# A four-layer graph kernel on one core: the last rows leave in four transfers, attention's bias sum may run on either of two engines, and the planner's search gets other settings

## The chip, the cores and the metric

The kernel runs on one core of a Trainium2 chip. The core has five engines with a queue of instructions each: TensorE (PE; its weight loads are shown as PEld), VectorE (DVE), ScalarE (ACT), GpSimd (POOL) and SyncE (SP), which here only issues DMA transfers. Each engine runs its queue in order and waits on semaphores for what other engines make. SBUF is the on-chip memory of 128 partitions, PSUM holds matmul results in eight banks. The metric is the device time of one execution in microseconds (us), the median over several runs.

## The reference

The input x holds 128 graphs of 64 nodes with 256 features in float32, adj an adjacency matrix per graph. Four layers follow one another; each adds its result to its input and normalises the rows.

```python
# layer 0, gated recurrent steps, l = 0..4; A = (adj != 0)
m = h @ weight[l];  agg = A^T @ m;  h = gru_cell(agg, h)
x = layernorm(x + h * mask)
# layer 1, two-layer perceptron with RMS norm
agg = epsilon * x + adj @ x
x = layernorm(x + silu(rmsnorm(agg @ W1 + b1) * w) @ W2 + b2)
# layer 2, hyperbolic: log map, sum over neighbours, exp map, projection
x = layernorm(x + project(expmap0(adj @ logmap0(x))))
# layer 3, attention over neighbours
h = x @ W_w^T + W_b
u = adj * exp(e_i + f_j + a_b);  a = u / sum(u)
x = layernorm(x + a @ h)
```

## The kernel before, in words

Two graphs share the 128 partitions as a block, four blocks make a group, and 16 groups make the input. A group's rows are a tile of 128 x 4 x 256. Three sets of buffers let groups overlap. The program of a group is written by `group(g)` (from L612) as a stream of operations, each with the engine, an estimated duration and the buffers that it reads and writes; a buffer may be split into parts such as the four blocks. Nothing is emitted there. A planner, `Flow`, orders the streams of all groups and then emits every instruction; it ties each to the one before it on its engine, so that the order of every queue is the plan's.

The planner keeps several plans at once. `advance` (L79) extends one plan until its TensorE clock passes a limit: at each step it looks at the first operations of up to four consecutive streams (`WINDOW`), works out when each could start, and takes the earliest. An operation with two ways (`either`, L180) stands in both engines' queues, and its key is its start plus what that way costs more than the cheapest:

```python
key = (t + o.ways[e][0] - min(w[0] for w in o.ways.values()) if len(o.ways) > 1 else t, *rank(s, o))
```

Equal starts are settled by a rank. There are three: the earlier stream first; the later stream first (loads aside); and a rank that weighs a stream's number by `LAG` against the operation's longest remaining path in its own stream (`way`). `issue` (L231) extends every kept plan by a stretch of `STRETCH` us with every rank, sorts the results by `bound()` (L133, an estimate of the time at which such a plan can end: TensorE's lost time plus all of its work, or the longest remaining path), and keeps the best `WIDTH` of them. When less than `ENDGAME` us of TensorE's work are left, stretches are half as long and three times as many plans are kept. The planner knows hops between engines, the eight banks and the DMA's rate. It has no term for one engine holding up another's access to memory, or for TensorE's clock.

The steps that the change and the prediction name are these. `layer_norm` (L668) takes row statistics per block (`st` L673, `mv` L674), adds epsilon (`ve` L676), raises to the power -1/2 on GpSimd (`rstd` L678), makes an offset (`off` L684) and writes the four blocks of the result with `scaled` (L352), each block on ScalarE (L354) or VectorE (L355). In layer 1, GpSimd adds the second bias to the rows (`xb`, L853, 128 x 1024 elements), the projection `ps_o` is the last large matmul work of a group, and `xb` L959 adds it to the rows. Layer 2 makes the logarithm's factor on VectorE with a series (L983), sums over neighbours (`ps_sup`), and adds the result (`y`, L1028). Layer 3 transposes the rows (`ps_T`), multiplies by the attention weights (`ps_a`), scales by the exponentials (`hw`, L1045 to L1050), adds the bias to the rows on VectorE (L1052, 128 x 1024 elements), multiplies with the adjacency (`ps_att`), and for each block divides by the sum (`rd`, L1058 to L1060) and adds to the rows (`y`, L1061). The last norm's four blocks leave in one transfer, issued by SP (L1065):

```python
dve(1030, lambda: nc.vector.tensor_add(x3.tile(), x3.tile(), over(wb_r.tile(), NB)), [x3], [x3, wb_r])
flow.op("SP", 0.1, lambda: nc.sync.dma_start(out_rows[g], o.tile()), (), [o])
```

Of the kernel before, what the change touches and what calls it, by code (L numbers as in the profile page):

```python
# [14 lines left out]
OP = mybir.AluOpType  # L15
# [128 lines left out]
class Flow:  # L144
# [15 lines left out]

    DMA = (2.0, 330.0, 1.0)
    TRANSFERS = 8
    WINDOW, STRETCH, WIDTH, LAG = 4, 25.0, 8, 40.0


    ENDGAME = 350.0

    BEHIND = mybir.DependencyInfo(mybir.DependencyClass.NoSync, mybir.DependencyReason.DATA)

# [60 lines left out]

    def issue(self):  # L231
        self.ways()
        ranks = (lambda s, o: (s, o.n), lambda s, o: (s if o.kb else -s, o.n), lambda s, o: (self.LAG * s - o.way, s, o.n))
        plans, until = [Plan(self)], 0.0
        while any(p.left for p in plans):
            late = until > self.work - self.ENDGAME
            until += self.STRETCH / 2 if late else self.STRETCH
            found = {}
            for p in plans:
                for rank in ranks:  # L240
                    c = p.copy()
                    if c.advance(until, rank):
                        found.setdefault((round(c.bound(), 3), c.left), c)
            plans = [found[k] for k in sorted(found)[:self.WIDTH * (3 if late else 1)]]
        p, parts = plans[0], []
        past = (p.past, p.order)
        while past is not None:
            parts.append(past[1])
            past = past[0]
        last = {}  # L250
        for part in reversed(parts):
            for eng, o in part:
                made = o.ways[eng][1]()
                for i in made if isinstance(made, list) else [made]:
                    if eng in last:
                        self.tc.add_manual_dep(i.ins, last[eng].ins.name, self.BEHIND, reason="the plan's order")
                    last[eng] = i
# [3 lines left out]
def kernel(  # L261
# [31 lines left out]
    nc = tc.nc  # L293
# [4 lines left out]
    NB = 4  # L298
# [4 lines left out]
    NG = B // G  # L303
# [9 lines left out]
    flow = Flow(tc)  # L313
# [27 lines left out]
    def dve(n, run, w, r):  # L341
        flow.op("DVE", 0.16 + 0.00105 * n, run, w, r)
# [18 lines left out]
    out_rows = out.rearrange("(g b t) n d -> g (t n) b d", b=NB, t=2)  # L361
# [11 lines left out]
    def over(t, n):  # L373
        return t.unsqueeze(1).to_broadcast([P, n, t.shape[-1]])
# [192 lines left out]
    def everywhere(v, n, name, t=None):  # L567
        t = t or fixed([P, n], name)
        flow.op("POOL", 0.55, lambda: nc.gpsimd.dma_start(
            t.tile(), bass.AP(tensor=v.tensor, offset=v.offset, ap=[[0, P], [1, n]])), [t], kb=n / 2)  # L570
        return t
# [3 lines left out]
    wb_r = everywhere(att_b, D, "wb_r")  # L575
# [36 lines left out]
    def group(g):  # L612
        s = g % NF

        def tiny(name, shape=(P, NB), dt=F32):
            t = f"{name}{s}"
            return Buf(lambda: small.tile(list(shape), dt, tag=t, name=f"{name}_{g}"), slot=(t, 2))
# [4 lines left out]
        def rows(tag, name):  # L622
            return u(tag, name, (P, NB, D))
# [44 lines left out]
        def layer_norm(y, tag, name, norm=None):  # L668

            st, mv = tiny("st", (P, NB, 6)), tiny("mv", (P, NB, 2))  # L670
            ve, rstd = tiny("ve", (P, 2, NB)), tiny("rstd", (P, 2, NB))
            for b in range(NB):
                dve(256, lambda b=b: nc.vector.bn_stats(st[:, b, :], y[:, b, :]), [(st, b)], [(y, b)])  # L673
                dve(4, lambda b=b: nc.vector.bn_aggr(mv[:, b, :], st[:, b, :]), [(mv, b)], [(st, b)])  # L674
            m = 2 if norm else 1
            dve(4, lambda: nc.vector.tensor_tensor(  # L676
                ve[:, :m, :], over(mv[:, :, 1], m), eps2[:, :m, :], OP.add), [ve], [mv])
            pool(1.1, lambda: nc.gpsimd.tensor_tensor(rstd[:, :m, :], ve[:, :m, :], pow2[:, :m, :], OP.pow), [rstd], [ve])  # L678
            if norm:
                dve(4, lambda: nc.vector.scalar_tensor_tensor(  # L680
                    norm.tile(), rstd[:, 1, :], float(np.sqrt(D)), rstd[:, 0, :], OP.mult, OP.mult), [norm], [rstd])
            o = rows(tag, f"x_{name}")
            off = tiny("off")
            dve(4, lambda: nc.vector.scalar_tensor_tensor(  # L684
                off.tile(), mv[:, :, 0], -1.0, rstd[:, 0, :], OP.mult, OP.mult), [off], [mv, rstd])
            for b in range(NB):
                scaled(256, lambda b=b: o[:, b, :], lambda b=b: y[:, b, :], lambda b=b: rstd[:, 0, b:b + 1],
                       lambda b=b: off[:, b:b + 1], [(o, b)], [(y, b), off, rstd])
            return o
# [18 lines left out]
        for t in range(2):  # L708
            q = quads[t]
# [122 lines left out]
        for n in range(2):  # L832
            ps = rows_of(hT, n)
            for j in range(2):
                b = 2 * n + j
# [5 lines left out]
        for t in range(2):  # L841
            q = quads[t]
# [17 lines left out]
        def chunk(c):  # L860
            return hid[c // 2][:, c % 2, :], [(hid[c // 2], (c % 2, n)) for n in range(2)]
# [76 lines left out]
        for c in range(KH):  # L938
            v, parts = chunk(c)
# [9 lines left out]
        for h in range(NB // 2):  # L949
            ps = bank("ps_o1")  # L950
            for j in range(2):
                b = 2 * h + j
# [4 lines left out]
            for j in range(2):  # L957
                b = 2 * h + j
# [38 lines left out]
        us = tiny("ss")  # L997
        sup = [bank("ps_sup") for _ in range(NB // 2)]
        for h in range(NB // 2):
            for j in range(2):  # L1000
                b = 2 * h + j
                pe(256, lambda b=b, j=j, ps=sup[h]: matmul(
                    ps[:, j * D:(j + 1) * D], adjT[:, b, :], tan[:, b, :], 0, 1), [sup[h]], [adjT, (tan, b)])
            for j in range(2):
                b = 2 * h + j
# [25 lines left out]
        x3 = layer_norm(y2, "B", "n2")  # L1031
# [8 lines left out]
        for b in range(NB):  # L1040
            ps = bank("ps_a")
            for k in range(KD):
# [6 lines left out]
                    hw[:, b, :D], ps[:, :D], AF.Identity, scale=hw[:, b, D:D + 1])),  # L1049
                ("DVE", 0.43, lambda ps=ps, b=b: nc.vector.tensor_scalar(  # L1050
                    hw[:, b, :D], ps[:, :D], hw[:, b, D:D + 1], None, OP.mult))], [(hw, b)], [ps, (hw, b)])
        dve(1030, lambda: nc.vector.tensor_add(x3.tile(), x3.tile(), over(wb_r.tile(), NB)), [x3], [x3, wb_r])  # L1052
        y3 = rows("y", "y3")
        rd = tiny("rd")
        for b in range(NB):
# [6 lines left out]
                y3[:, b, :], ps[:, :D], rd[:, b:b + 1], x3[:, b, :], OP.mult, OP.add),  # L1062
                [(y3, b)], [ps, (rd, b), (x3, b)])
        o = layer_norm(y3, "A", "n3")
        flow.op("SP", 0.1, lambda: nc.sync.dma_start(out_rows[g], o.tile()), (), [o])  # L1065

    for g in range(NG):
        flow.stream()
        group(g)
# [33 lines left out]
```

## Time and profile before

| | |
|---|---|
| median of 4 runs | 2431.53 us (2430.47 to 2432.34) |
| profiled execution, own time | 2432.88 us |
| its span, first to last instruction | 2431.1 us |
| TensorE busy | 2397.1 us (99%) |
| VectorE busy | 1892.3 us (78%) |
| ScalarE busy | 1148.0 us (47%) |
| GpSimd busy | 188.4 us (8%) |
| mean granted TensorE clock | 0.994 |
| transfers out | 16 of 512 KB, 2.9 us from issue to landing |

Times in the profile are counted from the start of the span. A line of the timeline gives start, duration, engine, line of the kernel, operation, output and inputs, shapes, and how many instructions were merged; in brackets stands how long the engine had been idle before it, and what ended that. An overlap of a few hundredths between neighbours on one engine is the pipelining of the records. The granted clock is the share of full speed that the throttle gave TensorE.

### The profile page before, as it was taken

The page shows a single profiled execution, that of the slowest core. Times are in us where ns is not written, and L with a number is a line of the kernel's source. Part 1 is how long each engine was busy: PE and PEld are TensorE (multiplying, and loading weights), DVE is VectorE, ACT ScalarE, POOL GpSimd, SP SyncE. Part 2 cuts the span into 40 slices and gives each one's busy share as a digit, 9 for nine tenths or more (in the row PEclk, how much of TensorE's full clock was granted, in tenths as well). Part 3 has the DMA queues.
Part 4 walks back from the last instruction along what each step waited for, and adds up shares of the span by engine and source line. Part 5 has one row for each costly group of instructions (what it writes and reads, how often), then busy time and mean ns, then how long its engine had stood idle before and what let it go on. Part 6 is the DMA issues. An engine that isn't in the chain of part 4 may idle for free.

```text
span 2431.1 us, 32703 instructions
## 1 busy us (share of the span) xinstructions
PE 2397.1 (99%) x12258; PEld 2104.9 (87%) x12258; DVE 1892.3 (78%) x4097; ACT 1148.0 (47%) x2408; POOL 188.4 (8%) x144
## 2 busy tenths in 40 slices
PE   9999999999999999999999999999999999999996
PEld 7888888888888888888888888888888888888864
DVE  3668787887888877778777887788787787878777
ACT  4434544444444444454444545455444544445453
POOL 4000000000100000000000100000000000000011
PEclk9999999999999999999999999999999999999997
DMA  4000000000000000000000000000000000000000
GB/s 127 3 1 12 1 29 1 18 12 1 29 1 27 3 18 11 1 27 3 17 13 1 29 1 27 3 20 10 1 29 1 18 12 1 27 9 18 9 9 18
DMA packets 39725, 36.21 MB, mean 15 GB/s; under 512 B 9956, under 2 KB 38656, under 8 KB 39568
## 3 DMA queue, kind: packets, MB, share of 16 engines
q1 hardware_dynamic: 37840, 32.25, 4.2%
q8 instruction: 97, 1.59, 0.3%
q10 hardware_dynamic: 1328, 1.31, 0.2%
q0 software_dynamic: 400, 0.57, 0.1%
q14 instruction: 60, 0.49, 0.1%
HBM read 25.74 MB, written 8.39 MB: 14 GB/s over the span
## 4 chain that ended last, share of the span: by engine, by line
PE 94%; DVE 4%; DMA 1%; ACT 1%; issue 0%; POOL 0%; ACTq 0%; POOLq 0%; SPq 0%; DVEq 0%
PE p_v L663 11%; PE p_w L663 11%; PE p_in L663 11%; PE p_r L663 11%; PE p_hn L663 11%; PE ps_o L333 9%; PE ps_agg L333 6%; PE p_u L663 6%; PE ps_hr L643 3%; PE ps_a L333 2%; PE p_wh L882 2%; PE p_vh L882 2%; PE p_1h L882 2%; PE ps_T L633 1%; PE ps_att L333 1%; PE p_uh L882 1%
## 5 line engine op out<-in xcount | busy, mean ns | idle before, releaser
L663 PE MATMUL p_hn<-hT,w_hn 128*128 128x256 f32 x1280 | 322.8, 380 | 0.0
L663 PE MATMUL p_in<-agg,w_in 128*128 128x256 f32 x1280 | 315.3, 379 | 0.0
L663 PEld LDWEIGHTS p_in<-agg,w_in 128*128 128x128 f32 x1280 | 240.2, 190 | 31.1
L663 PEld LDWEIGHTS p_hn<-hT,w_hn 128*128 128x128 f32 x1280 | 227.9, 191 | 22.7
L333 PE MATMUL ps_o<-w2s,hid 128*128 128x256 f32 x1024 | 231.2, 379 | 0.0
L333 PEld LDWEIGHTS ps_o<-w2s,hid 128*128 128x128 f32 x1024 | 193.9, 190 | 27.3 <-issue 1.2
L678 POOL TENSOR_TENSOR rstd<-ve,pow 128x4 f32<-128x4 f32 (+1 forms) x64 | 82.6, 1291 | 1492.1 <-DVE ve L676 1484.4
L767 ACT ACTIVATE V<-V,half_b 128x256 f32<-128x256 f32 x160 | 72.7, 499 | 199.1 <-DVE V L763 198.9
L663 PE MATMUL p_u<-tA,s 128*128 128x256 f32 x640 | 158.1, 381 | 1.4 <-DVE tA L746 0.6
L663 PE MATMUL p_w<-tA,s 128*128 128x256 f32 x640 | 158.1, 379 | 0.0
L663 PE MATMUL p_r<-hT,a 128*128 128x256 f32 x640 | 156.9, 379 | 0.0
L663 PE MATMUL p_r<-agg,a 128*128 128x256 f32 x640 | 156.7, 379 | 0.0
L663 PE MATMUL p_v<-tB,s 128*128 128x256 f32 x640 | 155.4, 379 | 0.0
L663 PE MATMUL p_v<-tB,na 128*128 128x256 f32 x640 | 154.5, 379 | 0.0
L663 PE MATMUL p_w<-hT,s 128*128 128x256 f32 x640 | 154.3, 379 | 0.0
L349 ACT COPY agg<-ps_agg 128x512 f32<-128x512 f32 x154 | 90.0, 585 | 114.1 <-PE ps_agg L333 98.8
L333 PEld LDWEIGHTS ps_agg<-edge,hr 128*128 128x128 f32 x1024 | 136.1, 191 | 6.6
L354 ACT ACTIVATE hnb<-p_hn,half_b 128x256 f32<-128x256 f32 x232 | 101.8, 473 | 81.4 <-PE p_hn L663 67.4
L333 PE MATMUL ps_agg<-edge,hr 128*128 128x128 f32 x1024 | 138.8, 275 | 0.0
L663 PEld LDWEIGHTS p_u<-tA,s 128*128 128x128 f32 x640 | 119.3, 190 | 21.0 <-DVE tA L746 2.3
L663 PEld LDWEIGHTS p_v<-tB,s 128*128 128x128 f32 x640 | 120.9, 190 | 16.3 <-PE ps_att L333 0.2
L663 PEld LDWEIGHTS p_w<-hT,s 128*128 128x128 f32 x640 | 120.7, 190 | 16.0
(233 smaller groups left out, 4688.0 us busy)
## 6 DMA issues: line engine op xcount, KB each, us to landing
x<-in_x_dram SPq DMA_DIRECT2D x16, 512.0 KB, 3.7
xr<-in_x_dram SPq DMA_DIRECT2D x16, 512.0 KB, 3.6
out_dram<-x_n SPq DMA_DIRECT2D x16, 512.0 KB, 2.9
edge<-in_adj_dram SPq DMA_DIRECT2D x32, 64.0 KB, 2.3
wm<-in_L_gnn_weight_dram SPq DMA_DIRECT2D x5, 256.0 KB, 5.2
w2s<-in_L_gnn_W_dram SPq DMA_DIRECT2D x1, 1024.0 KB, 10.0
w<-in_L_gnn_W_dram SPq DMA_DIRECT2D x2, 512.0 KB, 3.5
w_in_L_gnn_w_hh_dram<-in_L_gnn_w_hh_dram ACTq DMA_DIRECT2D x1, 512.0 KB, 5.5
```

The lines of the kernel that those rows point to most:

```text
L333: return nc.tensor.matmul(o, lhsT, rhs, start=(k == 0), stop=(k == nk - 1))
L349: flow.either([("ACT", 0.27 + 0.00077 * n, lambda: nc.scalar.copy(o(), i())), ("DVE", 0.16 + 0.00105 * n, lambda: nc.vector.tensor_copy(o( ...
L354: flow.either([("ACT", 0.27 + 0.00077 * n, lambda: nc.scalar.activation(o(), i(), AF.Identity, bias=bias(), scale=scale())), ("DVE", 0.16 ...
L633: turn(lambda j=j, c=c: nc.tensor.transpose(ps[:, c * HR + j * P:c * HR + (j + 1) * P], src[:, 2 * n + j, c * P:(c + 1) * P], ident.tile() ...
L643: turn(lambda j=j, c=c: nc.tensor.transpose(ps[:, j * D + c * P:j * D + (c + 1) * P], src[:, c, (2 * n + j) * P:(2 * n + j + 1) * P], iden ...
L663: pe(256, lambda c=c, k=k: nc.tensor.matmul(ps[:, c * HR:(c + 1) * HR], w[:, k, c * P:(c + 1) * P], v(k), start=first and c == k == 0, sto ...
L678: pool(1.1, lambda: nc.gpsimd.tensor_tensor(rstd[:, :m, :], ve[:, :m, :], pow2[:, :m, :], OP.pow), [rstd], [ve])
L767: act(256, lambda c=c: nc.scalar.activation(o[:, c, :], src(c), AF.Tanh, bias=half_b[:, i * KD + c:i * KD + c + 1], scale=0.5), [(o, c)], ...
L882: pe(256, lambda c=c: nc.tensor.matmul(ps[:, c * HR:(c + 1) * HR], w1f[:, w, (2 * q + c) * P:(2 * q + c + 1) * P], v[0](), start=first and ...
```

## The change

There are three parts. In the last group each of the four blocks leaves by a transfer of its own, which waits for that block only; the other groups' rows still leave in one. Attention's bias sum becomes an operation with two ways, VectorE (estimated at 1.24 us) or GpSimd (2.35 us), and the planner takes one of them for each group. In the search, the lag rank's weight becomes 60 (as a list with one entry), the number of plans 6, and the last part begins 200 us of TensorE work before the end, with stretches of 6 us and 32 plans.

```diff
-    WINDOW, STRETCH, WIDTH, LAG = 4, 25.0, 8, 40.0
-    ENDGAME = 350.0
+    WINDOW, STRETCH, WIDTH, LAGS = 4, 25.0, 6, (60.0,)
+    ENDGAME, LAST_STRETCH, LAST_WIDTH = 200.0, 6.0, 32
...
-        ranks = (lambda s, o: (s, o.n), lambda s, o: (s if o.kb else -s, o.n), lambda s, o: (self.LAG * s - o.way, s, o.n))
+        ranks = (lambda s, o: (s, o.n), lambda s, o: (s if o.kb else -s, o.n), *(lambda s, o, lag=lag: (lag * s - o.way, s, o.n) for lag in self.LAGS))
...
             late = until > self.work - self.ENDGAME
-            until += self.STRETCH / 2 if late else self.STRETCH
+            until += self.LAST_STRETCH if late else self.STRETCH
...
-            plans = [found[k] for k in sorted(found)[:self.WIDTH * (3 if late else 1)]]
+            plans = [found[k] for k in sorted(found)[:self.LAST_WIDTH if late else self.WIDTH]]
...
-        dve(1030, lambda: nc.vector.tensor_add(x3.tile(), x3.tile(), over(wb_r.tile(), NB)), [x3], [x3, wb_r])
+        flow.either([(e, us, lambda v=v: v.tensor_tensor(x3.tile(), x3.tile(), over(wb_r.tile(), NB), OP.add))
+                     for e, us, v in (("DVE", 1.24, nc.vector), ("POOL", 2.35, nc.gpsimd))], [x3], [x3, wb_r])
...
-        flow.op("SP", 0.1, lambda: nc.sync.dma_start(out_rows[g], o.tile()), (), [o])
+        for q in [slice(0, NB)] if g < NG - 1 else [slice(b, b + 1) for b in range(NB)]:
+            flow.op("SP", 0.1, lambda q=q: nc.sync.dma_start(out_rows[g, :, q, :], o[:, q, :]), (),
+                    [(o, b) for b in range(q.start, q.stop)])
```

## The prediction

> **What bounds the kernel now.** I read the page's first two parts, then busy time by stretches, then the waits of TensorE, then the last 130 us instruction by instruction.
>
> The page, busy time of each engine and the 40 slices of the span:
>
> ```profile
> PE 2397.1 (99%) x12258; PEld 2104.9 (87%) x12258; DVE 1892.3 (78%) x4097; ACT 1148.0 (47%) x2408; POOL 188.4 (8%) x144
> ...
> PE   9999999999999999999999999999999999999996
> ...
> PEclk9999999999999999999999999999999999999997
> ```
>
> TensorE works 2397.1 of 2431.1 us. All that an order of work can change is the other 34.0 us, and the matmuls that run at a lower clock. The view by stretches tells where those are (columns: stretch, its length, PE, PEld, DVE, ACT, POOL, granted clock, DMA):
>
> ```profile
> 1000.00:1400.00 400.00, 400.00 (x2080) 355.81 (x2079) 319.25 (x699) 195.07 (x413) 27.90 (x19) 1.00 0.04 14
> 1800.00:2200.00 400.00, 399.45 (x2071) 354.58 (x2070) 319.15 (x677) 191.28 (x397) 27.79 (x19) 1.00 0.04 12
> ...
> 2300.00:2350.00 50.00, 46.03 (x185) 30.35 (x184) 35.78 (x63) 26.64 (x49) 7.56 (x4) 0.97 0.04 11
> ```
>
> ```profile
> 2384.10:2402.10 18.00, 7.54 (x17) 5.05 (x16) 14.91 (x74) 8.44 (x27) 4.66 (x4) 0.67 0.00 1
> 2402.10:2417.80 15.70, 15.24 (x64) 12.59 (x64) 12.54 (x43) 9.26 (x23) 1.56 (x1) 0.83 0.00 1
> ```
>
> Between 200 and 2200 us TensorE idles 2.8 us in five stretches of 400; the first 50 us hold 3.0. From 2300 us on it idles 28: 4.0 up to 2350, 10.5 after its last projection (2384.1) up to 2402.1, 13.3 after its last matmul (2417.8). From 2384.1 on the last two groups run their hyperbolic step, attention and norms side by side, a chain of small VectorE steps: VectorE is busy 33.55 of the 40.4 us up to 2424.5, so 6.9 us of it are free. The clock drops to 0.67: the eight records of ps_sup take 3.75 us, where eight records of the same size take 1.73 us in mid-run.
>
> What made TensorE wait around 2305 and 2337, from the timeline:
>
> ```profile
> 2301.78 2.73 DVE L786 SCALAR_TENSOR_TENSOR hT<-V,hT 128x512 f32<-128x512 f32 x1
> ...
> 2333.73 3.44 DVE L870 TENSOR_TENSOR sqs<-sqs,sq 128x512 f32<-128x512 f32 x2
> ...
> 2305.38 0.63 PE L643 MATMUL ps_hr<-ident,hT 128*128 128x128 f32 x4 [1.44 <-DVE hT L788]
> ...
> 2337.92 4.33 PE L333 MATMUL ps_hid<-aggm,w 128*128 128x512 f32 x6 [2.53 <-DVE aggm L350]
> ```
>
> ```profile
> 2301.48 2.48 POOL L853 TENSOR_TENSOR xb<-x_n,b_r 128x1024 f32<-128x1024 f32 x1 [1.63 <-ACT x_n L354]
> ...
> 2333.95 2.67 POOL L853 TENSOR_TENSOR xb<-x_n,b_r 128x1024 f32<-128x1024 f32 x1 [1.75 <-DVE x_n L355]
> ```
>
> While GpSimd adds 128x1024 elements, a VectorE operation of 0.69 us takes 2.73, and a pair of 1.48 takes 3.44. All 4.0 us of TensorE's idling before 2350 follow from that. This bears on the change, which may put 16 more adds of that size on GpSimd. The two adds it is about, and the end:
>
> ```profile
> 2406.10 1.22 DVE L1052 TENSOR_TENSOR x_n<-x_n,wb_r 128x1024 f32<-128x1024 f32 x1
> 2406.63 1.56 POOL L678 TENSOR_TENSOR rstd<-ve,pow 128x4 f32<-128x4 f32 x1 [5.51 <-DVE ve L676]
> ...
> 2412.13 1.23 DVE L1052 TENSOR_TENSOR x_n<-x_n,wb_r 128x1024 f32<-128x1024 f32 x1 [0.21 <-PE ps_T L633]
> ...
> 2425.68 1.89 SPq L1065 DMA_DIRECT2D out_dram<-x_n  x2
> 2426.07 1.09 ACT L354 ACTIVATE x_n<-y,off,rstd 128x256 f32<-128x256 f32 x2 [0.42 <-DVE off L684]
> 2426.07 0.73 DVE L355 TENSOR_SCALAR x_n<-y,rstd,off 128x256 f32<-128x256 f32 x2
> ```
>
> **The base of the sum.** The profiled execution took 2432.88 us: a span of 2431.1 and 1.8 around it. The median of the four runs is 2431.53, 1.35 below. Differences are worked out inside the span and taken from the median.
>
> **Part 1, the last rows leave in four transfers.** Removed: one issue of 512 KB on SP that waits for all four blocks (ready 2427.16, issued 2427.2). Added: four issues of 128 KB, each behind its own block. The blocks end at about 2426.4 and 2426.8 (VectorE) and 2426.65 and 2427.16 (ScalarE). SP spends 0.389 us on an issue; in the best order it issues at 2426.4, 2426.8, 2427.2 and 2427.6, so the last starts 0.4 later than the one transfer did. A landing takes 2.9 us for 512 KB and 2.3 for the 64 KB of the edges; on the line between these, 128 KB takes 2.4, 0.5 less. Net -0.1. Bounds: -0.5 if only the size tells; +1.2 if the plan lists the slowest block first, so that three issues queue behind it. Nothing stands behind these on SP but the kernel's end.
>
> **Part 2, the bias sum on either engine.** VectorE's way is costed at 1.24 us (measured 1.22), GpSimd's at 2.35 (the like add took 2.36 to 3.29). The planner takes GpSimd when it could start more than 1.11 us before VectorE. In the first 14 groups the add hangs on no TensorE work, and VectorE is busy 80%: I cost it at nothing there. The cover is the other groups' matmuls: GpSimd's present add runs in mid-run too, and TensorE's waits on VectorE's L878, which it holds up, sum to 1.3 us over the run. If each new add did as much, +1.3; without cover, as at 2305 and 2337, about 2 us each. In the tail: the sum of the group ahead is ready at 2404.25 (its transposes are done) and runs at 2406.10, 1.85 late, so GpSimd would get it; from 2404.3 to 2406.7 it would hold up VectorE's ve (2406.02) by 0.65 us, and rstd would end near 2407.95 rather than 2408.19, since VectorE's add no longer stretches it from 1.01 to 1.56: -0.2. The last group's sum is ready at 2411.9 and starts at 2412.13, so it stays on VectorE: 0. On GpSimd (2412.0 to 2414.4) it would hold rd, L1060, which reads two tensors in SBUF, until 2414.4 where it now runs at 2413.46: +0.95. On GpSimd's queue rstd of the other group would stand behind the add and its wait for the transposes. Bounds for both tail sums: -2.45 (VectorE rid of both, nothing held) to +2.3 (each pays 2.37 for 1.22). I take -0.2, nearest to the rows at those places.
>
> The Trainium skill (SBUF — State Buffer, "SBUF: two separate sides") says that VectorE and GpSimd share a port pair as an exclusive lock, which a VectorE operation with two SBUF inputs holds or waits for as a whole. The trace agrees in 2.73 against 0.69 us. By that rule an add on GpSimd costs VectorE its full 2.36 us wherever a two-input operation comes next, so the sum of this part would be +2.3 rather than -0.2; rows speak for less, since matmul results from PSUM pass beside the add unhindered (L778 at 2115.69, inside an add from 2115.46 to 2117.83, keeps its 0.69).
>
> **Part 3, the search.** It writes the order of every queue anew. Up to 200 us before the end it keeps 6 plans and steps of 25 us (before: 8 plans, and from 350 us before the end 24 plans at 12.5); then 32 plans at 6 us. The lag rule weighs one group's lead at 60 us of remaining path, before 40.
> Mid-run: 2.8 us of idling in 2000. Bounds: none of it left, -2.8, or twice as much, +2.8. I take +0.3 for 6 plans instead of 8.
> Tail: I list the delays that the order alone makes. Idling behind GpSimd's add, 1.44 + 2.53 = 4.0. Then: xb waits for the other group's series (2384.1 to 2384.9), 0.8; y's first operation stands apart from the other three behind x_n (2402.0 to 2402.6), 0.6; x_n is ready at 2408.4 and ScalarE runs hw until 2409.6, 1.2; two stats of the group ahead run (2416.0 to 2416.9) before rd, 0.8; its other two hold up the last group's stats again, 1.1. That is 4.5, with the 4.0 altogether 8.5. From the last projection to the end the finer steps make seven choices instead of four. But the sum of these waits can't all go: VectorE has 6.9 free us there, and the two groups' work must be done by it. I take a third of 8.5 and round up: -3.0. Bounds: -8.5, and on the other side the lag below.
>
> Sum: -0.1 - 0.2 + 0.3 - 3.0 = -3.0, so 2428.5 us.
>
> **Rivals.** About 0.2% (4.9 us) is what a measurement of this kernel can tell from no change.
> *A, the forecast:* 2428.5, own range 2426.7 to 2431.5.
> *B, the finer tail takes most of the listed delays.* It counts as faster from 4.9 of 8.5 on. For it: five of the six are matters of what stands next in a queue. Against: the dearest, 4.0, comes from VectorE being held by GpSimd, and the planner has no term for that. At 7 of 8.5: 2424.5.
> *C, the last group falls behind.* The place is the run before 2384. Now its first norm (rstd) starts 32.3 us after that of the group ahead (2330.80 against 2298.46), and the last norms 1.4 apart. A lead valued at 60 instead of 40 can set it back by up to 20 us more, and this is now settled with 6 plans in 25 us steps. What TensorE can do meanwhile is the other group's sup, T, a and att: 32 records at 0.216 and 8 at 0.11, 7.8 us. Each us of setback beyond 7.8 is idle, up to +12.2. It counts as slower from 12.7 us of setback; at 14.5 it gives +6.7, 2438.2. Against: bound() counts a late group's remaining path, so the planner sees most of that.
> *D, GpSimd's adds eat the gain.* +2.3 in the tail and +1.3 in mid-run in place of part 2's -0.2, the rest of the sum as it is (-2.8): +0.8, 2432.3; within 0.2%.
>
> **How the numbers follow.** A 0.40, B 0.32, C 0.18, D 0.10. Faster by over 0.2% is B, 0.32; within is A and D, 0.50; slower is C, 0.18. The time is A's, 2428.5. The range goes from 2422.5 (B with all its 8.5, and part 1 at its best, reaches 2422.5) to 2437.5, which cuts off the worse part of C: about 0.13 outside. A's own range is 2426.7 to 2431.5.
>
> **What the changed profile would show.** Part 1: four issues of 128 KB at the end, the last one starting about 0.4 us after the last block, landings near 2.4 us. Part 2: some of the 16 sums as GpSimd operations of 2.4 us or more, and long two-input operations of VectorE beside them. Part 3: fewer us of TensorE idle between 2300 and 2417, a like 2.8 in mid-run, some 30 us of idling in all. Wrong would be: TensorE idle over 6 us in mid-run, a last group over 12 us further behind, or a tail from the last projection to the end longer than 47 us.

## The result, and the profile after

The changed kernel takes 2428.35 us (median of 42 runs, 2427.53 to 2430.09), the kernel before 2432.08 (60 runs, 2430.3 to 2432.99). The ratio is 0.9986 with a 95% interval of 0.9982 to 0.9991: some 3.4 us faster by the ratio and 3.7 by the medians, within the 0.2%. The profiled execution took 2429.03 us, with a span of 2427.1, 4.0 below that of the kernel before.

The view by stretches, with cuts at 200, 2100, 2300 us, then between, and at the end of the last projection, 2380.1 us (columns: stretch, its length, PE, PEld, DVE, ACT, POOL, granted clock, DMA share, GB/s):

```profile
200.00:2100.00 1900.00, 1897.20 (x9821) 1685.43 (x9820) 1522.30 (x3286) 903.13 (x1901) 129.12 (x90) 1.00 0.04 12
2100.00:2300.00 200.00, 200.00 (x1039) 178.15 (x1038) 156.12 (x320) 90.55 (x192) 10.15 (x7) 1.00 0.04 14
2300.00:2341.00 41.00, 38.86 (x163) 25.99 (x162) 30.47 (x58) 20.84 (x39) 8.46 (x5) 1.00 0.05 14
2341.00:2380.10 39.10, 38.98 (x167) 30.17 (x166) 33.52 (x79) 21.86 (x35) 2.65 (x2) 1.00 0.00 1
```

```profile
2380.10:2427.10 47.00, 21.28 (x80) 16.62 (x79) 33.63 (x138) 19.70 (x52) 12.45 (x9) 0.75 0.07 22
```

The last projection ends at 2380.1 us, 4.0 earlier than the 2384.1 of before. From there to the end it is 47.0 us, as before. So, taken together, the gain stands ahead of the tail. Inside the tail four differences cancel: the way from the last projection to the rows' transposes (ps_T) is 1.0 us shorter, the sixteen ps_a records behind them take 0.55 longer (5.90 against 5.35), the way from the last ps_att to the first transfer out 0.2 longer, and from there to the end 0.26 longer. Part of the 1.0 is one of the delays that the prediction lists: the last rows' xb started 0.8 us after its projection, behind the other group's series, and now VectorE waits for the projection.

```profile
2380.12 0.76 DVE L959 SCALAR_TENSOR_TENSOR xb<-ps_o,xb 128x256 f32<-128x256 f32 x2 [0.24 <-PE ps_o L333]
```

Over the whole span TensorE idles as long as before, 34.0 us; the 4.0 us are time of the same 12258 matmul records, 2397.1 us before:

```profile
PE 2393.1 (99%) x12258; PEld 2104.0 (87%) x12258; DVE 1896.6 (78%) x4104; ACT 1137.8 (47%) x2398; POOL 193.7 (8%) x147
```

Ahead of the tail the account closes. TensorE idles 6.0 us up to 2300 (before 5.85), and 2.3 from 2300 to the last projection (before 4.0): -1.5. The other -2.45 is matmul time: as many records (12179, before 12178) are busy for 2371.84 us where they took 2374.29. Most of that, 1.7, lies in the ten microseconds from 2335 on, where the granted clock had been 0.83 (six ps_hid records 1.5 us shorter, the ps_ss behind them 0.2); the rest was not located. The kernel before:

```profile
2335.00:2345.00 10.00, 7.47 (x23) 3.88 (x22) 4.22 (x5) 3.52 (x7) 2.64 (x2) 0.83 0.00 0
```

The changed kernel:

```profile
2335.00:2345.00 10.00, 9.56 (x31) 5.00 (x32) 5.94 (x11) 7.53 (x13) 1.02 (x1) 1.00 0.00 0
```

TensorE's timeline there shows why:

```profile
2333.05 1.02 PE L333 MATMUL ps_hid<-aggm,w 128*128 128x512 f32 x2
2335.44 2.81 PE L333 MATMUL ps_hid<-aggm,w 128*128 128x512 f32 x6 [1.37 <-DVE aggm L350]
```

```profile
2331.24 3.45 DVE L870 TENSOR_TENSOR sqs<-sqs,sq 128x512 f32<-128x512 f32 x2
```

GpSimd's add holds VectorE's pair of sums for 3.45 us as before, and TensorE waits for the same aggm. But one more projection of the other group (two records) stands behind the aggregation in the new order, so the wait is 1.37 us and not 2.53; and after it the six ps_hid records take 2.81 us where they took 4.33. GpSimd's add for the other group made TensorE wait 1.44 us for hT; now it makes it wait 0.61 for tA.

In the tail, both sums went to GpSimd, and of the earlier 14 only one did:

```profile
2399.36 2.35 POOL L1052 TENSOR_TENSOR x_n<-x_n,wb_r 128x1024 f32<-128x1024 f32 x1 [3.56 <-PE ps_T L633]
2401.01 0.73 DVE L676 TENSOR_TENSOR ve<-mv,eps 128x4 f32<-128x4 f32 x1
...
2407.70 2.36 POOL L1052 TENSOR_TENSOR x_n<-x_n,wb_r 128x1024 f32<-128x1024 f32 x1 [4.80 <-PE ps_T L633]
...
2408.34 1.73 DVE L1061 TENSOR_TENSOR rd<-rd,hw 128x1 f32<-128x1 f32 x1
```

ve takes 0.73 us and one rd 1.73, each until GpSimd's add is done, where their like take 0.16 (rd's line is L1060 in the kernel before).

At the very end SP issues five transfers:

```profile
2421.42 2.91 SPq L1068 DMA_DIRECT2D out_dram<-x_n  x5
...
2422.47 0.87 SPq L1068 DMA_DIRECT2D out_dram<-x_n  x1
2423.43 0.90 SPq L1068 DMA_DIRECT2D out_dram<-x_n  x2
```

```profile
2421.58 1.09 ACT L354 ACTIVATE x_n<-y,off,rstd 128x256 f32<-128x256 f32 x2 [0.19 <-DVE off L684]
```

The first line merges all five issues, the last line is the last two blocks on ScalarE. The third issue takes 0.87 us, the others 0.36 to 0.41. The last block is ready at 2422.67 and the last issue starts at 2423.93, 1.26 us later. From the first issue to the end of the span it is 5.68 us; in the kernel before, with two, 5.42.

### The profile page after: what moved, and what is told of

Its sections match the earlier page's. It is cut to its first block, busy times and chain, and to the rows that moved or that the text cites. A ratio compares the mean times of both kernels' runs of the same rounds, so it can differ in the third digit from the quotient of the medians.

```text
span 2427.1 us, 32711 instructions
## 1 busy us (share of the span) xinstructions
PE 2393.1 (99%) x12258; PEld 2104.0 (87%) x12258; DVE 1896.6 (78%) x4104; ACT 1137.8 (47%) x2398; POOL 193.7 (8%) x147
## 4 chain that ended last, share of the span: by engine, by line
PE 94%; DVE 5%; issue 0%; DMA 0%; ACT 0%; POOL 0%; POOLq 0%; SPq 0%; ACTq 0%; DVEq 0%
PE p_v L663 11%; PE p_w L663 11%; PE p_r L663 11%; PE p_in L663 11%; PE p_hn L663 11%; PE ps_o L333 9%; PE ps_agg L333 6%; PE p_u L663 6%; PE ps_hr L643 3%; PE ps_a L333 2%; PE p_wh L882 2%; PE p_vh L882 2%; PE p_1h L882 2%; PE ps_sup L333 1%; PE ps_T L633 1%; PE p_uh L882 1%
## 5 line engine op out<-in xcount | busy, mean ns | idle before, releaser
L354 ACT ACTIVATE hnb<-p_hn,half_b 128x256 f32<-128x256 f32 x243 | 107.0, 473 | 74.7 <-PE p_hn L663 56.0
L663 PEld LDWEIGHTS p_v<-tB,na 128*128 128x128 f32 x640 | 120.5, 190 | 16.0
```

Of the source, the lines that this page charges most:

```text
L354: flow.either([("ACT", 0.27 + 0.00077 * n, lambda: nc.scalar.activation(o(), i(), AF.Identity, bias=bias(), scale=scale())), ("DVE", 0.16 ...
L663: pe(256, lambda c=c, k=k: nc.tensor.matmul(ps[:, c * HR:(c + 1) * HR], w[:, k, c * P:(c + 1) * P], v(k), start=first and c == k == 0, sto ...
```

## The experiments

Medians of the kernel before on the same chip were 2431.9, 2432.03 and 2432.47 us in the three sets. Where "every queue as it is" is said, the planner ran with the changed kernel's (or the before kernel's) own costs, and only what the diff names was put elsewhere at emission; all other instructions stand in the same order on every engine. The diffs are shortened, comments in them are this document's. Line numbers in these runs' profiles are shifted by the lines that the edit adds.

### Part 1 undone: the last rows in one transfer

```diff
-            flow.op("SP", 0.1, lambda q=q: nc.sync.dma_start(out_rows[g, :, q, :], o[:, q, :]), (),
+            flow.op("SP", 0.1, lambda q=q: leave(q), (),   # leave: the last call sends the whole of o, the first three send nothing
                     [(o, b) for b in range(q.start, q.stop)])
```

> The changed kernel with every queue as it is, but the last group's rows leave in one transfer of 512 KB, issued behind the last block. By the prediction's working the four transfers end 0.1 us earlier than one: this kernel is 0.1 us slower than the changed one (some 2428.4 us, span 2427.2). Rival, the wire: in the changed kernel's trace 1 MB leaves at about 350 GB/s from the issue of the group ahead on, so the end is set by that and not by the last issue: 0.0, or 0.1 to 0.3 faster, since fewer issues stand before the last one. Third: the issues of 0.87 us in the changed kernel lie on the path: 0.5 faster.

Measured: 2427.83 us (2427.48 to 2428.79), ratio to before 0.9986 (0.9977 to 0.9995); span 2426.3.

```profile
2420.90 1.66 SPq L1074 DMA_DIRECT2D out_dram<-x_n  x2
```

From the first issue to the end 5.4 us, against 5.68 with four transfers. The four cost 0.26 us at the place where they work; the prediction had -0.1. The first issue itself comes 0.5 us earlier than in the changed kernel, ahead of anything that the edit touches: 0.42 of it are the sixteen ps_a records, which take 5.48 us here and 5.90 there, in the same order and behind the same wait. That much two executions differ, the two ratios to the kernel before are equal, and the medians' 0.5 can't be put down to the edit. By the 0.26 it is the second expectation that fits, 0.1 to 0.3 faster; whether the wire or the issues ahead of the last one make it, these runs don't separate.

### Part 2 undone: the sums on VectorE, same order

```diff
+        add = flow.either([...])            # planned as before: GpSimd for three of them
+        flow.swap[add] = "DVE", lambda: nc.vector.tensor_tensor(x3.tile(), x3.tile(), over(wb_r.tile(), NB), OP.add)
```

> The changed kernel with every queue as it is, but the three bias sums that the planner gave to GpSimd (one in mid-run, the two of the tail) stand in VectorE's queue at the place where the plan started them. If VectorE is held for as long as GpSimd adds: the long rd (1.73 us) falls to 0.16 and ve (0.73) to 0.16, VectorE does 2 x 1.22 instead; the first of the two lies beside a wait for hw, so the tail is 0.2 to 0.4 us shorter than in the changed kernel. Rival, GpSimd takes work off VectorE: the tail is 1.2 to 2.4 us longer, 2429.5 to 2430.8 us.

Measured: 2427.73 us (2426.95 to 2428.59), ratio 0.9983 (0.9974 to 0.9992); span 2425.6. In VectorE's timeline the sums take 1.21 and 1.22, and ve is back to its short time:

```profile
2399.46 1.21 DVE L1056 TENSOR_TENSOR x_n<-x_n,wb_r 128x1024 f32<-128x1024 f32 x1
2401.85 0.16 DVE L678 TENSOR_TENSOR ve<-mv,eps 128x4 f32<-128x4 f32 x1
2407.95 1.22 DVE L1056 TENSOR_TENSOR x_n<-x_n,wb_r 128x1024 f32<-128x1024 f32 x1
```

```profile
2419.94 2.91 SPq L1071 DMA_DIRECT2D out_dram<-x_n  x5
```

The rows' transposes (ps_T) start at 2397.10 against 2397.26, the first issue at 2419.94 against 2421.42: 1.3 us are won between the two. But not all of it is the edit's. The sixteen ps_a records behind the transposes, first in the changed kernel, then here, and then in the run further below that moves xb and leaves these sums on GpSimd:

```profile
2399.05 5.90 PE L333 MATMUL ps_a<-wattT,x3T 128*128 128x258 f32 x16
```

```profile
2398.89 5.07 PE L335 MATMUL ps_a<-wattT,x3T 128*128 128x258 f32 x16
```

```profile
2397.81 4.89 PE L343 MATMUL ps_a<-wattT,x3T 128*128 128x258 f32 x16
```

They follow one another without a gap, so 0.83 of the 1.3 us are matmul time at another clock (granted 0.62, 0.73 and 0.75 in these three), and the third, with the sums on GpSimd, is the shortest. The rest, 0.49, lies between the start of the last ps_att and the first issue, in VectorE's chain, which the long rd held up; 0.6 is the difference of the medians (the intervals of the two ratios overlap). The rival, by which GpSimd relieves VectorE, is out: the tail is shorter with the sums on VectorE, by a little more than the 0.2 to 0.4 worked out.

### Part 1 carried further: two groups leave in blocks

```diff
-        for q in [slice(0, NB)] if g < NG - 1 else [slice(b, b + 1) for b in range(NB)]:
+        for q in [slice(0, NB)] if g < NG - 2 else [slice(b, b + 1) for b in range(NB)]:
```

> The changed kernel, but the group before the last leaves in four transfers of 128 KB too, so its first block can leave some 0.7 us earlier. If the 1 MB on the wire sets the end: 0.4 to 0.7 us faster than the changed kernel, 2427.8. If SP's issues set it (eight of 0.39 to 0.9 us in a row): 0.5 to 2 us slower.

Measured: 2429.02 us (2428.06 to 2430.03), ratio 0.9989 (0.998 to 0.9997); span 2427.7: some 0.7 us slower than the changed kernel. From the first issue (2421.01) to the end 6.69 us. The rate falls from some 345 GB/s to some 265; the view of the transfers has these rows of rates for the kernel with eight small transfers, in slices of 0.425 us from 2415 us:

```profile
GB/s 0 0 0 0 0 0 0 0 0 0 0 0 0 0 0 0 267 253 263 251 251 270 287 287 256 84 0 0 0 19 0 0 0 0 0 0 0 0 0 0
```

and for the changed kernel, with four:

```profile
GB/s 0 0 0 0 0 0 0 0 0 0 0 0 0 0 0 0 0 231 347 347 345 345 335 342 176 0 0 0 0 0 0 0 19 0 0 0 0 0 0 0
```

The issues tell why:

```profile
2421.01 3.79 SPq L1068 DMA_DIRECT2D out_dram<-x_n  x8
...
2423.42 1.39 SPq L1068 DMA_DIRECT2D out_dram<-x_n  x3
...
2424.41 0.40 SPq L1068 DMA_DIRECT2D out_dram<-x_n  x1
```

```profile
2421.85 1.09 ACT L354 ACTIVATE x_n<-y,off,rstd 128x256 f32<-128x256 f32 x2 [0.18 <-DVE off L684]
```

SP issues the eight one behind the other, 0.45 to 0.50 us apart (each takes 0.36 to 0.40), and 128 KB every 0.49 us are 267 GB/s, about the rate seen. The last block is ready at 2422.94, the last issue starts 1.47 us later. So it is the second expectation that came: SP's issues set the end, not what the wire can carry. In the changed kernel, where one of five transfers is large, the rate stays at 345.

### The wait behind GpSimd's add taken out of the kernel before

```diff
-        pool(2.35, lambda: nc.gpsimd.tensor_tensor(xb.tile(), x1.tile(), over(b2_r.tile(), NB), OP.add), [xb], [x1, b2_r])
+        add = flow.op("POOL", 2.35, ...)     # planned as it was
+        if g >= NG - 2:                      # emitted four VectorE operations later, on VectorE
+            flow.swap[add] = "DVE", lambda: nc.vector.tensor_tensor(xb.tile(), x1.tile(), over(b2_r.tile(), NB), OP.add), 4
```

> The kernel before with every queue as it is, but the last two groups' bias add xb (L853) goes from GpSimd to VectorE, four VectorE operations later, where VectorE waits for TensorE or has time. If GpSimd's add held up VectorE and so TensorE: the waits of 1.44 us (for hT) and 2.53 us (for aggm) fall to 0 and about 0.6, the clock stays at 1.00 between 2335 and 2345 us, so that another 1.7 us go, and the kernel ends 4 to 5 us earlier, at 2427 to 2428 us. Rival, the waits come from VectorE's own order: no change beyond 0.5 us, or 1.2 slower for the added VectorE work.

Measured: 2428.2 us (2426.76 to 2428.82), ratio 0.9985 (0.9977 to 0.9994); span 2426.7, 4.4 below the kernel before.

```profile
2303.89 0.60 PE L653 MATMUL ps_hr<-ident,hT 128*128 128x128 f32 x4
...
2334.74 2.81 PE L343 MATMUL ps_hid<-aggm,w 128*128 128x512 f32 x6 [0.88 <-DVE aggm L360]
```

The wait for hT is gone, that for aggm is 0.88 (0.6 was expected), the six records take 2.81 us, and the clock from 2335 to 2345 us is 1.00. By its medians the kernel is 3.7 us faster, a little less than the 4 to 5 expected. Moving two adds of the old kernel, with no other instruction in another place, brings as much as the whole change. That settles where this time was in the kernel before.

### The same in the changed kernel, and all three together

```diff
         # the changed kernel, every queue as it is; for g >= NG - 2:
+        flow.swap[add] = "DVE", lambda: nc.vector.tensor_tensor(xb.tile(), x1.tile(), over(b2_r.tile(), NB), OP.add), 4
```

> The changed kernel with every queue as it is, but the last two groups' xb goes to VectorE, four of its operations later, as was done to the kernel before (3.7 us there). If the search's gain was the shorter wait behind GpSimd's add and the clock that stays up: here only the waits that are left go, 0.61 and 1.37 us, so 1 to 2 us (2426.5 to 2427.5 us), and both kernels end within 1.5 us of each other. If the search's gain came from elsewhere: 3.5 us again, 2424.8 us.

Measured: 2426.72 us (2426.3 to 2427.92), ratio 0.9979 (0.9971 to 0.9988). It brings 1.6 us here where it brought 3.7 in the old kernel: what was left of the same wait. (The last projection ends 1.3 us earlier here, and 4.9 in the old kernel.) The two kernels then end 1.5 us apart (2428.2 and 2426.72), where 1.5 was the bound expected.

```diff
         # xb as just above, the sums as in part 2 undone, the last rows as in part 1 undone
+        flow.swap[add] = "DVE", lambda: nc.vector.tensor_tensor(xb.tile(), x1.tile(), over(b2_r.tile(), NB), OP.add), 4
...
+        flow.swap[add] = "DVE", lambda: nc.vector.tensor_tensor(x3.tile(), x3.tile(), over(wb_r.tile(), NB), OP.add), 0
```

> The changed kernel with every queue as it is, but xb of the last two groups late on VectorE, all bias sums on VectorE, and the last rows in one transfer. If the three costs are apart from one another: 1.5 + 0.6 + 0.3 us faster than the changed kernel, 2426 us, and faster than both kernels. If VectorE in the tail is too full for the sums once the waits ahead are gone: no faster than with xb alone.

Measured: 2425.74 us (2425.28 to 2426.22), ratio 0.9977 (0.9968 to 0.9987): xb late on VectorE, all sums on VectorE, and one transfer, in the changed kernel's order. It is 2.6 us faster than the changed kernel by the medians, where 2.4 was expected, and faster than both kernels.

### The settings of the search, one by one

Part 3 alone on the kernel before:

```diff
-    WINDOW, STRETCH, WIDTH, LAG = 4, 25.0, 8, 40.0
-    ENDGAME = 350.0
+    WINDOW, STRETCH, WIDTH, LAGS = 4, 25.0, 6, (60.0,)
+    ENDGAME, LAST_STRETCH, LAST_WIDTH = 200.0, 6.0, 32
```

> The kernel before with part 3 alone: bias sums on VectorE, the last rows in one transfer, the search planned anew with the new settings. If the search brought the gain and parts 1 and 2 cost a little (0.3 and 0.6 us by the first runs): 3.5 to 5 us faster than the kernel before, 2427 to 2428.5 us. Rival, the gain needs the sums' second way, by which the tail is planned: within 1 us of the kernel before. Rival, it is the luck of one plan: anything from 5 faster to 5 slower.

Measured: 2434.32 us (2433.07 to 2435.59), ratio 1.001 (1.0002 to 1.0019): slower. In this order one group finishes far ahead (the two transfers are issued 14.4 us apart), and TensorE waits for the other:

```profile
2370.94 16.52 PE L333 MATMUL ps_o<-w2s,hid 128*128 128x256 f32 x64 [2.76 <-DVE hid L946]
...
2413.28 1.94 PE L633 MATMUL ps_T<-ident,x_n 128*128 128x128 f32 x8 [10.16 <-DVE x_n L355]
```

Parts 1 and 2 alone, with all the old settings:

```diff
-    WINDOW, STRETCH, WIDTH, LAGS = 4, 25.0, 6, (60.0,)
-    ENDGAME, LAST_STRETCH, LAST_WIDTH = 200.0, 6.0, 32
+    WINDOW, STRETCH, WIDTH, LAGS = 4, 25.0, 8, (40.0,)
+    ENDGAME, LAST_STRETCH, LAST_WIDTH = 350.0, 12.5, 24
```

> The changed kernel with the old search settings (8 plans, lag 40, from 350 us before the end 24 plans at 12.5 us), so parts 1 and 2 alone. If parts 1 and 2 bring nothing: 0 to 1 us slower than the kernel before, 2431.5 to 2433 us, with the waits of TensorE behind GpSimd's add near 2305 and 2337 us much as there. If the sums on GpSimd relieve VectorE: 1 to 2.5 us faster. If their place in mid-run matters: TensorE's idling between 200 and 2200 us grows from 2.8 to over 4 us.

Measured: 2446.71 us (2444.87 to 2447.77), ratio 1.0061 (1.0048 to 1.0074). The last projection ends at 2398.6 only. TensorE idles 10.2 us up to 2300 (3.6 of them from 200 to 2100, so mid-run is a little worse too), and then 7.5 up to there, with waits such as the one below. The sums' place in mid-run is not what costs: five of them went to GpSimd there, and the idling from 200 to 2200 us is 3.7, under the 4 that was named, while two runs below have none there and idle 5.7 and 5.6.

```profile
2389.18 9.44 PE L333 MATMUL ps_o<-w2s,hid 128*128 128x256 f32 x36 [4.42 <-DVE hid L946]
```

The changed kernel with the lag's weight back at 40:

```diff
-    WINDOW, STRETCH, WIDTH, LAGS = 4, 25.0, 6, (60.0,)
+    WINDOW, STRETCH, WIDTH, LAGS = 4, 25.0, 6, (40.0,)
```

> The changed kernel with the lag rank's weight back at 40. If the weight of 60 is what makes the good order: near the run with all old settings, over 5 us slower than the changed kernel. If the finer end is: within 2 us of the changed kernel, 2426.5 to 2430.5. If each setting only draws another plan: some other place between 2426 and 2447, and a tail from the last projection to the end that is not 47 us.

Measured: 2438.8 us (2435.02 to 2440.8), ratio 1.0026 (1.0014 to 1.0038). It is neither near the run with all the old settings, 8 us away, nor within 2 us of the changed kernel.

The changed kernel with the old end of the search and 8 plans (the weight stays 60):

```diff
-    WINDOW, STRETCH, WIDTH, LAGS = 4, 25.0, 6, (60.0,)
-    ENDGAME, LAST_STRETCH, LAST_WIDTH = 200.0, 6.0, 32
+    WINDOW, STRETCH, WIDTH, LAGS = 4, 25.0, 8, (60.0,)
+    ENDGAME, LAST_STRETCH, LAST_WIDTH = 350.0, 12.5, 24
```

> The changed kernel with the old end of the search (from 350 us on 24 plans at 12.5 us, 8 plans before) and the new weight of 60. If the finer end is what brings the gain: over 5 us slower than the changed kernel. If the weight is: within 2 us of it. If each setting only draws another plan: anything between 2426 and 2447.

Measured: 2435.87 us (2434.69 to 2436.54), ratio 1.0015 (1.0006 to 1.0025). Taken alone, 7.5 us slower than the changed kernel also fits "the finer end brings the gain"; the other runs don't.

The changed kernel with 8 plans instead of 6, and nothing else:

```diff
-    WINDOW, STRETCH, WIDTH, LAGS = 4, 25.0, 6, (60.0,)
+    WINDOW, STRETCH, WIDTH, LAGS = 4, 25.0, 8, (60.0,)
```

> The changed kernel with 8 plans instead of 6 in the long first part of the search, the smallest of the changes of settings. If the settings act by what they are meant to do: within 1 us of the changed kernel, or faster, since more plans are kept. If each setting only draws another plan: a difference of 2 us or more to either side, made between 2300 us and the end.

Measured: 2432.96 us (2431.82 to 2433.46), ratio 1.0003 (0.9993 to 1.0013). Keeping two more plans costs all of the gain. That the difference is over 2 us was expected of a new plan; that more than half of it lies before 2300 was not: TensorE idles 8.65 us up to there instead of 6.0.

Put side by side, in us; the columns behind the median are from each profiled execution, the end of the last projection from TensorE's timeline:

| kernel | median | idle up to 2300 | last projection ends | from there to the end |
|---|---|---|---|---|
| before | 2432.08 | 5.85 | 2384.1 | 47.0 |
| changed | 2428.35 | 6.0 | 2380.1 | 47.0 |
| part 3 alone | 2434.32 | 5.9 | 2387.5 | 45.6 |
| parts 1 and 2 alone | 2446.71 | 10.2 | 2398.6 | 45.3 |
| weight 40 | 2438.8 | 9.25 | 2391.0 | 46.5 |
| old end, 8 plans | 2435.87 | 8.85 | 2387.6 | 47.2 |
| 8 plans | 2432.96 | 8.65 | 2383.4 | 48.0 |
| before, xb late | 2428.2 | 6.1 | 2379.3 | 47.4 |
| changed, all three edits | 2425.74 | 5.7 | 2378.1 | 45.4 |

The last column stays between 45.3 and 48.0 in all of them, whatever the order (up to 1 us of that can be the clock of the ps_a records, as seen above); the one before it goes from 2378 to 2399 and decides the time. No single setting carries the gain: taking back the weight, the number of plans, or that number together with the finer end loses 4.6 to 10.5 us against the changed kernel, and giving them all to the old kernel loses 2.3. (The finer end was not taken back by itself.) Neither "the finer end does it" nor "the weight does it" fits all of them; that each setting draws another order, and the changed kernel's is the best of the six drawn here, does. That is what is left, not what was traced: why the planner ranks these orders as it does was not tried.

## Why the prediction was right or wrong

The time and its sign were right, 2428.5 against 2428.35, in the case A that was held likeliest. The way there was only partly right, and that the number came out so near is luck: by the profiled executions the four terms -0.1, -0.2, +0.3 and -3.0 came as about +0.3, +0.5, +0.15 and -4.9. Two had the wrong sign, and the last one's excess paid for them.

**Part 1, -0.1: wrong in size and sign.** Measured +0.26 at its place. The step that failed is the last issue, worked out to start 0.4 us after the last block: it started 1.26 after it, since one issue took 0.87 us and not 0.389. The shorter way from the last issue to the end made good most of that, 3.17 us against 4.13 with one transfer, 1.0 where the working had 0.5. The landings themselves were as worked out, 2.4 us in the median. The bound of +1.2 held.

**Part 2, -0.2: wrong.** The forecast that the last group's sum stays on VectorE failed, since it was read from the old order's readiness, and the order was new; both went to GpSimd. The price was named, though: "+0.95" for an rd held until GpSimd is done came as 1.57 more on rd and 0.57 more on ve, inside the bound of +2.3, and putting the sums back wins 0.6 in the median and 0.5 in the trace. It was a cost, not a gain. The Trainium skill (SBUF — State Buffer, "SBUF: two separate sides") has the lock as exclusive and for the whole instruction; the trace agrees, 1.73 against 0.16 us. That mid-run costs nothing held too: one sum went to GpSimd there, and the idling from 200 to 2100 us is 2.80 us, where it was 2.79.

**Part 3, mid-run +0.3: about right.** +0.15 up to 2300 us. But it was luck: in four of the five runs with other settings TensorE idles 2.8 to 4.3 us more up to 2300 than in the kernel before. In the stretch that the bound of +2.8 was made for, 200 to 2200 us, they idle 0.8 to 2.9 more, and the largest passes it.

**Part 3, tail -3.0: the right place, too small, and by another mechanism.** The list of delays had two halves. The 4.0 us behind GpSimd's add was the right place: there TensorE's waiting went from 4.0 to 2.0. But the working summed idle time alone, and TensorE's idling over the whole span stayed at 34.0 us, where the prediction looked for some 30. What went is matmul time: 2.45 us ahead of the last projection's end, of which 1.7 are matmuls that no longer run at the lower clock, and 1.5 behind it, where the first ps_sup follows the projections at once and takes 1.89 us, not 3.75. That was the term left out; 2.53 us of idling had been priced at 2.53. (The prediction set 3.75 us against 1.73 for eight records; 1.73 is their spacing, and a line that merges eight at full clock reads 1.89.) Of the 4.5 us of queueing behind the last projection the new order took some 1.2: 1.0 ahead of ps_T, and 0.3 behind the last ps_att once the sums are back on VectorE. Parts 1 and 2 and slower ps_a records used that up, so that the tail is 47.0 us before and after. And the finer steps are not what won the 4.0, as part 3 alone at +2.3 and the runs with one setting taken back show. "A third of 8.5" was a number that the outcome happened to meet.

**The rivals.** B asked for 4.9 us of the delays, and the change did not get to that: 2.0 and 1.2. "The dearest comes from VectorE being held, and the planner has no term for it" was true, and an order can still dodge half of it by chance. All 4.0 us were put down to GpSimd's add; moving it in the kernel before leaves 0.88 of the wait for aggm, so that 3.1 are shown to be. C happened in part 3 alone: the groups' transfers are 14.4 us apart, 13 more than before. At C's price that is some 5 us of idling; the run is 2.3 us slower. D's price was right in kind, some 0.5 us in the tail and not 2.3, and hid under the gain. The chance of 0.18 for a time over 0.2% slower was low for what a new order can do: of six combinations of these settings, other than the kernel before, one is faster than it, one within its interval, four slower, two of these by over 0.2% (1.0026 and 1.0061).

## What to carry to other kernels

Where a planner writes the order, a change to its settings or to one operation's choices is a new draw, and the sum to make is the spread of the draws; undo the settings one at a time before crediting one. Look for what the planner's costs leave out and remove that by hand: here two adds moved from GpSimd to VectorE won as much as the new search did. A wait of TensorE is to be priced with the matmuls behind it, which may run slower for some microseconds; here the idling stayed the same, and the matmuls' own time made the whole difference.

## What the runs showed of the hardware that was not expected

After 2.53 us of idling in the kernel before, six ps_hid records take 4.33 us; after 1.37 or 0.88 us the same six take 2.81. The length of the last wait alone does not decide: in the tail of the kernel before, ps_sup takes 3.75 us after a wait of 1.70, and in that kernel with xb moved it takes 1.97 after 1.84. Nor does the order: in the changed kernel and the five runs that keep its order on TensorE, the same sixteen ps_a records, 1.8 us behind the same wait of 4.6, take from 4.89 to 5.90 us, with granted clocks of 0.75 and 0.62.

A VectorE operation of 128x1 elements can be held as long as a large one: rd, 0.16 us by itself, took 1.73 beside GpSimd's add of 128x1024.

Eight transfers of 128 KB were issued by SP some 0.49 us apart and went at about 265 GB/s; one of 512 KB and four of 128 went at about 345, and one of their issues took 0.87 us. Why that one did was not tried.
